# Layer 1 of a two-layer gated network: output stage ordered behind expert parts, per-query products in a narrower window, the last group's first expert products in five PSUM banks

## The chip, the cores and the metric

The kernel runs on one core of a Trainium2 chip. The metric is the device time of one execution in microseconds. A measured time is the median of the runs given; the profile is one further execution.

## The reference

64 sequences of 128 tokens by 128 features, with a context of 77 by 128 each, pass through two layers of gated cross attention and a mixture of eight experts. Cut to what matters here, the second layer is:

```python
x = x + tanh(g_xattn[1]) * L1_xattn(layernorm(x), ctx, ctx, ...)
x = x + tanh(g_ffn[1])   * L1_ffn(layernorm(x), Wg, W1, W2)

def L1_xattn(query, key, value, ...):        # 16 heads of 8
    scores = einsum('bhqd,bhkd->bhqk', q, k) + einsum('bhqd,qkd->bhqk', q, rel_k)
    attn = softmax(scores / sqrt(8))
    out = einsum('bhqk,bhkd->bhqd', attn, v) + einsum('bhqk,qkd->bhqd', attn, rel_v)
    return out @ Wo + bo

def L1_ffn(x, Wg, W1, W2):                   # 8 experts, hidden 256, top 2
    combine = ...                            # the two best probabilities, normalised
    h = square(relu(einsum('td,edh->teh', x, W1)))
    return einsum('te,ted->td', combine, einsum('teh,ehd->ted', h, W2))
```

Everything is float32 with tight accuracy, so matrix products with the experts' weights are made from a high and a low part.

## The kernel before, in words

The sequences go in 16 groups of four. In layer 1 each group passes through a pipeline whose stages lie in successive steps of one loop (`run`, L1120): step k runs the output stage (`l1_out`) and then the routing (`l1_route`) of group k-2, the attention proper (`l1_attend`) of group k-1, the projections (`l1_project`) and the per-query position products (`l1_relate`) of group k, and beside them the experts' parts (`l1_ffn`, through `tape`) of an earlier group.

The stages are Python generators. `weave` (L42) interleaves them: each stream has a row in `PLAN` with a window (start and end as shares of the step), a priority, and an entry "behind". Streams marked "experts" leave a mark after every part; a stream with a number n as its "behind" gets order edges, so that its TensorE instructions stand behind the experts' part n+1 marks back. An order edge is no semaphore wait; it only binds the order in which the scheduler may place instructions on TensorE. The program so traced goes through a scheduler that fixes the order of every engine's queue at build time with its own model of durations. On the chip each engine takes its queue in order, and so does SP, which issues most DMAs.

What the prediction touches, in the order in which the data of a group flows:

- `l1_rel` (L779): 32 queries by four, per-query products of q with the position table, in six chunks of two banks. ACT copies each bank to sg (L785) and stores it to DRAM (ra, L786).
- `l1_fetch` (L799): SP reads the products back, turned, as rq: four transfers per sequence, 16 per group.
- `l1_attend`: scores (L824) plus rq on DVE (L826), maximum (L827), subtraction on POOL (L828), transposes to the bank ST (L836), exp on ACT (L837), weighing by the values (L844). After all of them the relative-value products L884, in four chunks, each copied to rvs by DVE (L888). SP stores rvs to DRAM (rd, four transfers, L892) and reads it back as rp (L894).
- `l1_out`: the residual x is loaded (L903) and bo added on POOL (L904); rp is transposed on TensorE into po (L908), the rest of the attention is added (L910), divided (L912), transposed (L916) and projected (L922).
- `l1_project`: q, k and v products (L719) for the next group; `split3` makes three bfloat16 pieces; `stack_q` and `stack_k` store them (dq, L150; dk, L155) and SP reads them back as qst (L735) and kst (L747).
- `l1_ffn`: per expert two first products pz (L165 to L167 from L985, each product in three matmuls), squared relu (L988 to L992), high and low part (ACT L995, POOL L996), the expert's scores spread over the partitions (pb, L608) and copied to sb by ACT (L613), the second product py, and its sum (L622, L623). First products have two banks (tag "gu"); pb and py share one bank (tag "y"). The copy sb and the bank "misc" have one buffer each. At a group's end `flush` (L587 to L589) turns the sum and stores it.

Of the kernel before, what the change touches and what calls it, by code (L numbers as in the profile page):

```python
# [10 lines left out]
F32 = mybir.dt.float32  # L11
# [8 lines left out]
B, S, D = 64, 128, 128  # L20
# [21 lines left out]
def weave(tc, streams, marks=None):  # L42
# [31 lines left out]
    wei=(0, 0.7, 0, 6),  # L74
    max=(0.05, 0.8, 1000, None),
    fea=(0.2, 0.6, 500, None),
    out1=(0.25, 0.4, 600, None),
    att1=(0.1, 0.95, 0, None),
    rel1=(0.37, 0.93, 0, None),
    relT=(0.6, 0.9, 500, None),  # L80
    relL=(0.5, 0.8, 500, None),
    prj1=(0, 0.35, 0, None),
    t0=(0, 1.1, 0, "experts"),
    t1=(0, 1.15, 0, "experts"),
    attE=(0, 0.35, 500, None),
    tE=(0.1, 1.1, 0, "experts"),
    prjT=(0, 0.55, 1000, None),
# [7 lines left out]
class Spare:  # L95


    def __init__(self, pool, bufs):
        self.pool, self.bufs = pool, bufs

    def tile(self, shape, dt, tag, name):
        return self.pool.tile(shape, dt, tag="gu", bufs=self.bufs, name=name)


class Net:
# [496 lines left out]
        nc.scalar.copy(s3[:24], pp[:24, :GT])  # L602
        return s3

    def spread(self, w, s3):

        pb = self.pY.tile([128, 512], F32, tag="y", name="pb")
        self.nc.tensor.matmul(pb, lhsT=w, rhs=s3, start=True, stop=True)  # L608
        return pb

    def score_in(self, s3, e):
        sb = self.fp.tile([128, GT], F32, tag="sb", bufs=1, name="sb")
        self.nc.scalar.copy(sb, self.spread(self.sel[:, e : e + 1].to_broadcast([128, 128]), s3))  # L613
        return sb

    def add_expert(self, e, acc, py, sb):
# [314 lines left out]
    def l1_route(self, s):  # L931
# [32 lines left out]
        s["sd"] = self.scores_out(p)  # L964
        yield

    def l1_ffn(self, g, s):
        nc, a = self.nc, self.fp
        x3, xh, xl, sd = s["x"], s["xh"], s["xl"], s["sd"]
        acc = a.tile([128, GT], F32, tag="acc", bufs=2, name="acc")  # L970

        def down(e, hs):
            sb = self.score_in(sd, e)
            py = self.pY.tile([128, 512], F32, tag="y", name="py")
            for c, (m, hh, hl) in enumerate(hs):
                self.mm3(py, self.w2s[0][:, m], self.w2s[1][:, m], hh, hl, start=(c == 0), stop=(c == 1))
            self.add_expert(e, acc, py, sb)

        late = None
        for e in range(E):  # L980
            hs = []
            for c in range(2):
                m = slice((2 * e + c) * 128, (2 * e + c + 1) * 128)
                pz = self.pGU.tile([128, 512], F32, tag="gu", bufs=self.gub, name="pz1")
                self.mm3(pz, self.w1s[0][:, m], self.w1s[1][:, m], xh, xl)  # L985
                t = a.tile([128, GT], F32, tag="t", bufs=3, name="t")

                nc.scalar.activation(t, pz, AF.Relu)  # L988
                if c:
                    nc.vector.tensor_tensor(t, t, t, ALU.mult)  # L990
                else:
                    nc.scalar.activation(t, t, AF.Square)  # L992
                hh = a.tile([128, GT], F32R, tag="hh", bufs=3, name="hh")
                hl = a.tile([128, GT], F32R, tag="hl", bufs=3, name="hl")
                nc.scalar.copy(hh, t)  # L995
                nc.gpsimd.tensor_tensor(hl, t, hh.bitcast(F32), ALU.subtract)  # L996
                hs.append((m, hh, hl))
                yield
                if late:
                    down(*late)  # L1000
                    late = None
                    yield
                if e == 1 and c == 1:
                    self.flush()
            late = (e, hs)
        down(*late)
        self.pending = (acc, x3, self.out[4 * g : 4 * g + 4].rearrange("b p d -> p b d"))
        yield
# [147 lines left out]
    def next_layer(self):  # L1156

        tc = self.tc
        for cm in self.f0_open:
            cm.__exit__(None, None, None)  # L1160
        self.f0_open = None
        s2 = self.ctx1.enter_context(tc.tile_pool(name="psS2", bufs=1, space=PSUM))
        self.pGU = self.ctx1.enter_context(tc.tile_pool(name="psg1", bufs=1, space=PSUM))
        self.gub = 2
        self.banks = itertools.cycle(((self.pS, "S"), (s2, "S2"), (self.pST, "ST")))
        self.l1_ffn_setup(self.ctx1.enter_context(tc.tile_pool(name="f1", bufs=1)))
        self.ppcm, self.pp = self.pool("p1")
        self.l1_buffers(4)
# [87 lines left out]
```

## Time and profile before

| | |
|---|---|
| median of three runs | 2787.84 us (2786.68 to 2804.19) |
| profiled execution, its own time | 2781.41 us |
| its span, first to last instruction | 2779.7 us |
| mean granted TensorE clock | 0.934 |
| TensorE matmul, busy | 2403.1 us (86%) |
| VectorE (DVE), busy | 1949.9 us (70%) |
| ScalarE (ACT), busy | 1561.4 us (56%) |
| GpSimd (POOL), busy | 1545.5 us (56%) |
| chain that ended last, by engine | PE 49%, DMA 17%, DVE 15%, issue 6%, POOL 5%, SP queue 4%, ACT 3% |

The busy time of TensorE is modelled from pipelined matmuls, so a high share is no proof that TensorE is the bound. The chain that ended last is followed back from the last instruction, at each step to whatever released it; transfers have 17% of it. Layer 0 lasts to about 1340 us. Layer 1 follows, with steps of 76 to 84 us from about 1785 to 2575 us, and a tail in which the last groups have no other work beside them (from about 2690 us TensorE is busy 55 us of 80).

### The profile page before, as it was taken

The numbers are of one execution on the slowest core, as the hardware profiler recorded it, in microseconds if no ns is written. First come the engines' busy times: TensorE is split into PE (matmuls) and PEld (weight loads), VectorE is DVE, ScalarE is ACT, GpSimd is POOL, SyncE is SP. The second block draws the span as 40 slices with busy tenths as digits, with TensorE's granted clock in tenths as the row PEclk, the third lists the DMA queues.
The fourth block names the chain that finished last, engine by engine and source line by source line (L and its number), as shares of the span: only waits on it lengthen the run. The fifth ranks groups of instructions, "written<-read, shape, count | busy, mean of one in ns | idle before, by whom it ended". The sixth has DMA issues, their size and how long they took to land.

```text
span 2779.7 us, 61119 instructions
## 1 busy us (share of the span) xinstructions
PE 2403.1 (86%) x23638; PEld 1655.3 (60%) x23638; DVE 1949.9 (70%) x4054; ACT 1561.4 (56%) x3030; POOL 1545.5 (56%) x1508
## 2 busy tenths in 40 slices
PE   3788998898998998899886988889989888889876
PEld 2456666666666666666564555566666565656654
DVE  3378888888888888888764656656656666656566
ACT  2455655565655555565543545556656565656556
POOL 4455555555545565554645646655645665655556
PEclk9989999999999999999996899989999999999999
DMA  6744445534445534432434745565554566664510
GB/s 146 167 113 84 105 85 112 115 93 104 106 84 112 118 95 99 112 87 58 99 67 132 140 92 119 122 123 115 108 113 106 115 125 125 125 125 103 99 27 8
DMA packets 504414, 290.57 MB, mean 105 GB/s; under 512 B 264614, under 2 KB 480814, under 8 KB 504027
## 3 DMA queue, kind: packets, MB, share of 16 engines
q1 hardware_dynamic: 476475, 246.28, 43.8%
q10 hardware_dynamic: 27648, 40.38, 4.0%
q8 instruction: 186, 3.05, 0.5%
q14 instruction: 105, 0.86, 0.1%
HBM read 147.19 MB, written 138.60 MB: 103 GB/s over the span
## 4 chain that ended last, share of the span: by engine, by line
PE 49%; DMA 17%; DVE 15%; issue 6%; POOL 5%; SPq 4%; ACT 3%; DVEq 0%; POOLq 0%; ACTq 0%
PE py L165 4%; PE py L166 3%; DMA kst<-dk 3%; PE py L167 3%; PE ST L836 3%; DMA rp<-rd 3%; PE AV L385 2%; PE AV L844 2%; PE pg L165 2%; PE S L779 2%; DMA rq<-ra 2%; PE pu L165 2%; PE pg L166 2%; PE pg L167 2%; DVE sc L826 2%
## 5 line engine op out<-in xcount | busy, mean ns | idle before, releaser
L524 POOL TENSOR_TENSOR hl<-t,hh 128x512 fp32r<-128x512 f32 x336 | 442.8, 1321 | 362.5 <-ACT hh L523 348.9
L996 POOL TENSOR_TENSOR hl<-t,hh 128x512 fp32r<-128x512 f32 x256 | 347.1, 1368 | 219.9 <-ACT hh L995 216.6
L523 ACT CAST hh<-t 128x512 fp32r<-128x512 f32 x336 | 207.3, 617 | 175.4 <-PE py L167 74.2
L828 POOL TENSOR_TENSOR sc<-sc,mx 128x308 f32<-128x308 f32 x256 | 187.4, 737 | 189.6 <-DVE mx L827 145.0
L516 ACT ACTIVATE t<-pg 128x512 f32<-128x512 f32 x336 | 201.0, 598 | 151.0 <-PE pg L167 105.5
L517 DVE SCALAR_TENSOR_TENSOR t<-t,pg 128x512 f32<-128x512 f32 x336 | 227.9, 678 | 75.1 <-ACT t L516 74.5
L613 ACT COPY sb<-pb 128x512 f32<-128x512 f32 x256 | 150.0, 586 | 192.3 <-PE pb L608 191.5
L518 DVE TENSOR_TENSOR t<-t,pu 128x512 f32<-128x512 f32 x336 | 227.5, 677 | 14.9 <-PE pu L167 6.3
L837 ACT ACTIVATE rel<-ST 77x512 f32<-77x512 f32 x256 | 158.4, 619 | 123.6 <-PE ST L836 120.4
L826 DVE TENSOR_TENSOR sc<-S,rq 128x308 f32<-128x308 f32 x256 | 119.9, 473 | 153.3 <-PE ST L836 57.1
L622 DVE TENSOR_TENSOR ys<-sb,py 128x512 f32<-128x512 f32 x224 | 152.7, 682 | 86.3 <-PE py L167 80.9
L995 ACT CAST hh<-t 128x512 fp32r<-128x512 f32 x256 | 156.8, 625 | 58.9 <-PE py L167 48.4
L836 PE MATMUL ST<-ident,sc 128*128 128x128 f32 (+1 forms) x1024 | 171.5, 293 | 16.0 <-ACT rel L837 6.3
L399 ACT ACTIVATE P<-ST 77x512 f32<-77x512 f32 x256 | 151.0, 591 | 55.9 <-PE ST L396 53.4
L165 PE MATMUL pg<-xh,wg_h 128*128 128x512 f32 x336 | 160.4, 477 | 15.0 <-DVE t L518 13.9
L165 PE MATMUL py<-hh,wd_h 128*128 128x512 f32 x336 | 156.6, 466 | 18.9 <-ACT sb L613 12.5
L358 DVE TENSOR_REDUCE mx<-S 128x5 f32<-128x385 f32 (+1 forms) x192 | 110.3, 577 | 78.5 <-PE S L355 77.4
L165 PE MATMUL pu<-xh,wu_h 128*128 128x512 f32 x336 | 159.2, 474 | 5.8 <-DVE t L517 5.6
L988 ACT ACTIVATE t<-pz 128x512 f32<-128x512 f32 x256 | 151.4, 597 | 22.4 <-POOL hl L996 21.1
L836 PEld LDWEIGHTS ST<-ident,sc 128*128 128x128 f32 (+1 forms) x1024 | 123.4, 149 | 56.3 <-issue 13.4
L785 ACT COPY sg<-S 128x385 f32<-128x385 f32 (+1 forms) x192 | 91.6, 515 | 114.0 <-PE S L779 108.1
L166 PE MATMUL py<-hl,wd_h 128*128 128x512 f32 x336 | 147.8, 440 | 2.1 <-POOL hl L524 2.1
(248 smaller groups left out, 6582.8 us busy)
## 6 DMA issues: line engine op xcount, KB each, us to landing
rq<-ra SPq DMA_DIRECT2D x256, 154.0 KB
qst<-dq SPq DMA_DIRECT2D x96, 384.0 KB
ra<-sg ACTq DMA_DIRECT2D x128, 192.5 KB
kst<-dk SPq DMA_DIRECT2D x96, 231.0 KB
dq<-f SPq DMA_DIRECT2D x47, 384.0 KB
od<-av SPq DMA_DIRECT2D x32, 512.0 KB
ra<-sg ACTq DMA_DIRECT2D x64, 231.0 KB
dq<-f SPq DMA_DIRECT2D x47, 256.0 KB
```

The costliest lines, as they stand in the source:

```text
L165: nc.tensor.matmul(ps, lhsT=wh, rhs=xh, start=start, stop=False)
L166: nc.tensor.matmul(ps, lhsT=wh, rhs=xl, start=False, stop=False)
L516: nc.scalar.activation(t, pg, AF.Tanh, scale=0.5)
L517: nc.vector.scalar_tensor_tensor(t, t, 1.0, pg, ALU.add, ALU.mult)
L518: nc.vector.tensor_tensor(t, t, pu, ALU.mult)
L523: nc.scalar.copy(hh, t)
L524: nc.gpsimd.tensor_tensor(hl, t, hh.bitcast(F32), ALU.subtract)
L826: nc.vector.tensor_tensor(sc, sp[:, :, :KL], rqs[b][:, hg], ALU.add)
L828: nc.gpsimd.tensor_tensor(sc, sc, m.unsqueeze(2).to_broadcast([128, 4, KL]), ALU.subtract)
L836: nc.tensor.transpose(st[:r, j, :], sc.rearrange("q j k -> q (j k)")[:, j * KL : j * KL + r], self.ident)
L837: nc.scalar.activation(relg[:KL, hg, b], st[:KL].rearrange("k j (q e) -> k j q e", e=2), AF.Exp, scale=1.0 / math.sqrt(HD))
L996: nc.gpsimd.tensor_tensor(hl, t, hh.bitcast(F32), ALU.subtract)
```

## The change

Three rows of the plan are altered. The output stage (`out1`) gets order edges behind the experts' parts (its "behind" goes from none to 2). The window of the per-query products (`rel1`) ends at 0.78 of the step and not at 0.93. The window of the experts' parts (`t1`) ends at 1.25 and not at 1.15. For the last group alone, the first expert products rotate over the two "gu" banks and the three banks that the attention used (S, S2, ST), and the spread of the scores goes to the bank "misc" and not to the bank "y" that the second products use.

```diff
-    out1=(0.25, 0.4, 600, None),
+    out1=(0.25, 0.4, 600, 2),
-    rel1=(0.37, 0.93, 0, None),
+    rel1=(0.37, 0.78, 0, None),
-    t1=(0, 1.15, 0, "experts"),
+    t1=(0, 1.25, 0, "experts"),
...
-    def __init__(self, pool, bufs):
-        self.pool, self.bufs = pool, bufs
+    def __init__(self, pool, bufs, tag="gu"):
+        self.pool, self.bufs, self.tag = pool, bufs, tag
     def tile(self, shape, dt, tag, name):
-        return self.pool.tile(shape, dt, tag="gu", bufs=self.bufs, name=name)
+        return self.pool.tile(shape, dt, tag=self.tag, bufs=self.bufs, name=name)
...
-    def spread(self, w, s3):
-        pb = self.pY.tile([128, 512], F32, tag="y", name="pb")
+    def spread(self, w, s3, last=False):
+        pool, tag = (self.pmisc, "misc") if last else (self.pY, "y")
+        pb = pool.tile([128, 512], F32, tag=tag, name="pb")
...
+    def zbank(self, g):
+        return next(self.tailz) if g == self.ng - 1 else Spare(self.pGU, self.gub)
...
-            sb = self.score_in(sd, e)
+            sb = self.score_in(sd, e, g == self.ng - 1)
...
-                pz = self.pGU.tile([128, 512], F32, tag="gu", bufs=self.gub, name="pz1")
+                pz = self.zbank(g).tile([128, 512], F32, tag="gu", name="pz1")
...
+        gu = Spare(self.pGU, self.gub)
+        self.tailz = itertools.cycle((gu, Spare(self.pS, 1, "S"), gu, Spare(s2, 1, "S2"), gu, Spare(self.pST, 1, "ST")))
```

More of the change, by code (lines that the diff above doesn't have):

```diff
@@ L603, in scores_out, with score_in @@
         return s3
-    def spread(self, w, s3):
-        pb = self.pY.tile([128, 512], F32, tag="y", name="pb")
+    def spread(self, w, s3, last=False):
+        pool, tag = (self.pmisc, "misc") if last else (self.pY, "y")
+        pb = pool.tile([128, 512], F32, tag=tag, name="pb")
         self.nc.tensor.matmul(pb, lhsT=w, rhs=s3, start=True, stop=True)
         return pb
-    def score_in(self, s3, e):
+    def score_in(self, s3, e, last=False):
         sb = self.fp.tile([128, GT], F32, tag="sb", bufs=1, name="sb")
-        self.nc.scalar.copy(sb, self.spread(self.sel[:, e : e + 1].to_broadcast([128, 128]), s3))
+        self.nc.scalar.copy(sb, self.spread(self.sel[:, e : e + 1].to_broadcast([128, 128]), s3, last))
         return sb
```

## The prediction

> **What bounds the kernel now.** I read the page's shares first: TensorE is busy 86% of the span and the chain that ended last names several engines and DMA, so no single engine is the bound and the stage has to be asked. Only the second layer is touched (the first ends near 1340 us), so the next view is TensorE's waits in its steady part, eleven steps from 1770 to 2640 us. Columns: engine and line, what it waited for, total us, times, longest.
>
> ```profile
> PE po L908 <- DMA rp<-rd: 56.1, 11, 7.0
> PE S L824 <- DVE sc L826: 11.6, 13, 1.3
> PE pp L599 <- POOL p3b L138: 10.3, 11, 1.0
> PE S L824 <- DVE avt L855: 6.2, 11, 0.6
> ```
>
> One wait stands out: 56.1/11 = 5.1 us per step in which TensorE stands before the output stage's first transposes (L908), because the relative-value result rp is not back from DRAM. The timeline of TensorE shows it in one step:
>
> ```profile
> 2255.03 0.60 PE L836 MATMUL ST<-ident,sc 128*128 128x128 f32 x4
> 2261.19 1.11 PE L908 MATMUL po<-ident,rp 128*128 128x128 f32 x4 [5.56 <-DMA rp<-rd]
> ```
>
> Why rp is late is in SP's queue in that step (start, time taken, line, transfer, count):
>
> ```profile
> 2230.68 7.42 SPq L799 DMA_DIRECT2D rq<-ra  x10
> ...
> 2241.46 4.84 SPq L892 DMA_DIRECT2D rd<-rvs  x4
> ...
> 2254.03 0.79 SPq L894 DMA_DIRECT2D rp<-rd  x1
> 2254.86 1.63 SPq L735 DMA_DIRECT2D qst<-dq  x2
> 2258.88 2.38 SPq L747 DMA_DIRECT2D kst<-dk  x2
> ```
>
> SP takes one transfer after another. I measure from T0, the end of the step's last relative-value product (L884; 2235.0 here). The score fetches (rq) start at T0-4.3, the stores of the product (rd) go out at T0+6.5, rp is asked for at T0+19.1 and is there at T0+26.2. Over the eleven steps that end with the L908 at 1785.7 to 2575.5, rp is there 26.1 to 28.6 us after T0, mean 26.9, and a step is 78 us long.
>
> **The change, part by part.** The diff only shifts planner numbers; the built order of each engine's instructions tells what moves.
>
> *Output stage behind the experts.* In a steady step of before, 120 TensorE instructions lie between the last L884 and L908; in the changed order 87, in twelve steps alike. L908 moves forward, against what the words suggest. It loses 14 split products (0.235 us start to start in the timeline: 3.3), 2 projections (0.55 each for 308 columns: 1.1), 8 score transposes (0.13: 1.0), 4 weighing products (0.4), 4 score products (0.3), 1 score spread (0.3): 6.4 us of cover. Before, TensorE needs 20.7 us from T0 to L908, 1.0 of it waits; so it would arrive 13 to 14 us after T0. The 6.4 us of work are not gone, they follow L908. So a step changes by 6.4 us plus the shift of rp's landing against T0: break-even is a landing at T0+26.9-6.4 = T0+20.5.
>
> *Per-query products closer together.* They (L779) now end earlier against T0: the order puts 64 more L884 products (2 x 1.08 us), 6 split products of py (1.45), 3 of pz (0.75), a q projection (0.97) and smaller work between them and T0, 13.9 us by the rows' start-to-start times, against 5.5 before. The last two chunks' copies to sg (0.49 each) and the stores to ra (0.35; 3.3 from issue at 2227.36 to the first rq) follow, so the rq fetches start about 5 us after the last L779, at T0-8.9 instead of T0-4.1. That is the gain. On SP, however, the queue order changes too. From the first rq to rd: before 14 transfers, 10.8 us, 0.77 each; after 19 (12 rq, 3 dq, the output store, 3 dk), 14.6 us. Then rd and x (4.9 + 0.5), and now both qst and both kst go ahead of rp (1.6 + 2.4). rp is asked for at T0-8.9+24.0 = T0+15.1, four us earlier than before, but behind 1.2 MB of qst and kst. In the trace's DMA records of the step at 2254, the packets of qst (1,536 of 512 B) pass from 2257.9 to 2264 and those of kst (1,536 of 308 B) up to 2268, in queue order and with all engines full: 10 us, beginning 3 us after the issue. With qst asked for at T0+11.1, rp can pass at T0+24 and is there at about **T0+25**. From below: rp 5.0 us after its issue, as in the step at 2646.8 with nothing behind it: T0+20. From above: SP no faster per transfer than before (0.89 over 27) and 7.7 us to land plus the queue: T0+28. I take 25 because the packets' order is seen.
>
> TensorE's wait then grows from 5.1 to some 11 us, and a step gains 25 - 26.9 + 6.4 = **+4.5 us** (bounds -0.5 and +7.5). What hides behind that wait costs nothing: POOL's addition of bo (L904) is now ahead of seven other POOL operations and waits for x, asked for between the rd stores at T0+8 and there 4.75 us later (2252.49 to 2257.24 before); with L904's 1.26 and the four or five POOL operations that TensorE needs before L908 (0.7 to 1.3 each) it can't be at L908 before about T0+19; the DVE copies of L884's results now stand behind the k split (L135, L137), under half a us. The granted clock is 0.50 in 2258 to 2264 around the wait, and also around waits of only 3.3 us (1869 to 1875), so that loss stays in both kernels: 0.
>
> Twelve steps have this order; the step after it (no next projection; 17.4 us to L908, no wait before) loses the same 6.7 us of cover with 16 rq ahead of rd, so I count it as the thirteenth: 13 x 4.5 = +58 us.
>
> The Trainium skill ("DMA: Bandwidth & Descriptors", "Anatomy of one DMA") gives a transfer about 2 us plus its bytes over 436 GB/s, fitted on another issue path; for rp's 256 KB that would be an estimated 2.6 us, a landing at T0+17.7 and a change of some -40 us in all. The trace speaks against it for this place: rp takes 4.9 to 7.7 us from issue to use in the steps of full size.
>
> *Last group's products in five banks, its score spreads in another bank.* This touches only the last 40 us. There TensorE pays, per expert, a spread and the wait for its copy:
>
> ```profile
> 2767.13 0.38 PE L608 MATMUL pb<-s,sel 128*128 128x512 bf16 x1 [0.85 <-DVE ys L622]
> 2768.18 0.50 PE L165 MATMUL py<-hh,w2s_h 128*128 128x512 f32 x1 [0.68 <-ACT sb L613]
> ```
>
> From spread to spread 3.56 us (2767.13 to 2770.69). With the spread in its own bank 0.38 + 0.68 = 1.06 us can leave this chain, at most 8 x 1.06 = 8.5. But POOL has two subtractions (1.28 to 1.7) and half an addition per expert, some 3.5 us, which is late next while first products remain. The five banks end waits of 0.3 to 1.0 us on ACT (L988) that POOL would then hold. I take **-5 us** (-1 to -9).
>
> Sum: +58 - 5 = +53 us on the profiled execution's own 2781.41 us (span 2779.7 and 1.7 around it). The three timed runs' median, 2787.84, lies 6.4 above; the difference carries over: **2841 us**.
>
> **Rivals.**
> *The earlier fetches win (not slower).* The rq fetches begin 4.8 us earlier against T0 and four of them move behind rp. If DMA catches up while TensorE works, rp lands at or before T0+20.5, and from there on the step is not longer. For it: DMA share is only 0.45 to 0.8 at 2243 to 2255, so there is room; at 2646.8 rp lands at T0+17.3. Against it: that step has no qst and kst ahead. At T0+20 the steps give 13 x (-0.5) = -7, with the tail -12: 2776; with the other small waits (28 us in the view above) half gone, about 2765.
> *Partly so.* rp at T0+21 to 22: 13 x 0.5 to 1.5 less 5: +2 to +15, 2790 to 2803.
> *SP and DMA both slow.* With 12 rq, 3 dq and 3 dk in a row the queue is full when rd comes; rp at T0+28: 13 x 7.5 - 5 = +93, 2881.
> *The change does what it says.* L908 is covered and the 5.1 us go: 13 x -5.1 - 5 = -71, 2717. The built order speaks against it, since L908 has less work ahead of it, not more; only a landing at T0+15 would do it.
>
> **How the numbers follow.** Forecast (rp at T0+23 to 27, +26 to +80 us with the tail) 0.62; partly 0.12; earlier fetches win 0.12, half of it beyond 1%; slow queue 0.12; as said 0.02. About 1% (28 us) is what a measurement of this kernel can tell from no change. Slower by over 1%: forecast, nearly whole, and slow queue, 0.73. Faster by over 1%: 0.08. The rest, 0.19, within. The range, from the not-slower bound of the steps (2776) to the slow queue (2881) with the tail's 4 us on either side: 2772 to 2885.
>
> **What would show it.** TensorE's wait at the output stage's first transposes: 8 to 13 us per step instead of 5.1, arriving under 20 us after the last L884; SP with both qst and kst ahead of rp; a step of about 82 us; the last group's experts at about 3 us instead of 3.56. I am wrong if rp lands under 20 us after the last L884, or if a wait in the denser per-query products (on ACT's sg copies) is larger than the one at rp.

## The result, and the profile after

| | before | after |
|---|---|---|
| median of the timed runs | 2795.11 us (4 runs, 2786.68 to 2804.19) | 2831.03 us (4 runs, 2824.06 to 2834.84) |
| profiled execution, its own time | 2781.41 us | 2834.84 us |
| its span | 2779.7 us | 2833.1 us |
| mean granted TensorE clock | 0.934 | 0.929 |
| TensorE matmul, busy | 2403.1 us (86%) | 2417.5 us (85%) |
| DMA in the chain that ended last | 17% | 22% |
| SP's queue in that chain | 4% | 8% |

The ratio is 1.0125, with a 95% interval of 1.0079 to 1.0171: the changed kernel is slower by 22 to 48 us. The two profiled executions lie 53.4 us apart, more than the medians (35.9 us): the one before is 5 us under the lowest of its four timed runs, the one after is the highest of its four. Of the 53.4 us, 8.2 are there before the first L908 of layer 1 (1496.3 against 1504.5 us), in code that the change doesn't touch. That is scatter: the order of every engine up to that point is the same in both traces, and the profiled executions of six kernels below, which don't alter it either, reach it at 1494.0 to 1503.2 us. So 45 us belong to layer 1: 49.7 us more from the first use of rp to the last (1198.5 against 1248.2 us), and 4.5 us less from there to the end (84.9 against 80.4 us). Of the 49.7 us, 33.0 lie in the ten steady steps that follow here, 6.4 ahead of them and 10.3 behind them, where TensorE waits 9.0 us for rp at 2694.9 and before waited none.

The steady steps, from one first use of rp to the next, take 79.0 us before (ten steps, 1785.7 to 2575.5) and 82.3 us after (ten steps, 1800.3 to 2623.0). TensorE's waits in these steps of the changed kernel (columns as before: what waited, for what, total us, times, longest; lines from L780 on have moved by one):

```profile
PE po L909 <- DMA rp<-rd: 75.4, 11, 9.1
PE S L885 <- DVE avt L856: 21.3, 10, 2.6
PE S L825 <- DVE sc L827: 8.0, 20, 0.6
PE ST L837 <- POOL sc L829: 5.0, 3, 3.7
```

The wait for rp has grown from 5.1 to 6.9 us a step. Beside it stands a new one, 2.1 us a step at the relative-value products (L885). The wait at pp (L599, 10.3 us before) is gone from this list.

One step on TensorE and on SP, by their timelines (start, time taken, line, operation, in brackets the idle time and what ended it). T0, the end of the last relative-value product, is 2191.7 here:

```profile
2184.50 2.15 PE L885 MATMUL S<-rel,rv 128*32 128x64 f32 x66 [2.62 <-DVE avt L856]
...
2205.21 0.48 PE L845 MATMUL AV<-rel,vb 128*32 128x128 f32 x8
2212.17 1.12 PE L909 MATMUL po<-ident,rp 128*128 128x128 f32 x4 [6.48 <-DMA rp<-rd]
```

```profile
2176.52 4.54 SPq L800 DMA_DIRECT2D rq<-ra  x8
...
2192.61 1.50 SPq L893 DMA_DIRECT2D rd<-rvs  x2
...
2195.51 1.97 SPq L893 DMA_DIRECT2D rd<-rvs  x2
2197.51 3.20 SPq L736 DMA_DIRECT2D qst<-dq  x2
2200.76 1.79 SPq L748 DMA_DIRECT2D kst<-dk  x2
2202.66 2.47 SPq L895 DMA_DIRECT2D rp<-rd  x1
```

The score fetches start 15 us ahead of T0 instead of 4, rd goes out at T0+1, rp is asked for at T0+11.0 and used at T0+20.5. But it is asked for behind qst and kst, and the time from its request to its use is 9.5 us, where before it was 6.1 to 7.7 us.

The windows of the same step (stretch, its length, busy time of TensorE, weight load, DVE, ACT, POOL with counts, then the granted clock, the DMA share and GB/s) show what surrounds the two waits:

```profile
2183.00:2186.00 3.00, 1.50 (x56) 1.50 (x60) 2.17 (x7) 0.52 (x1) 1.09 (x2) 0.64 1.23 217
2186.00:2189.00 3.00, 3.00 (x25) 2.25 (x16) 1.61 (x3) 0.52 (x1) 0.83 (x2) 0.50 1.26 221
...
2207.00:2210.00 3.00, 0.00 (x0) 0.00 (x0) 0.00 (x0) 0.00 (x0) 1.09 (x2) 0.62 1.20 142
2210.00:2213.00 3.00, 0.83 (x5) 0.83 (x5) 0.00 (x0) 0.00 (x0) 0.00 (x0) 0.50 1.29 174
2213.00:2216.00 3.00, 3.00 (x16) 1.68 (x14) 2.26 (x3) 0.62 (x1) 1.90 (x2) 0.50 0.42 57
```

Between 2207 and 2212 all four compute engines are nearly idle while the DMA share is 1.20 and more (a packet counts with all its time in the stretch where it starts, so the share can pass 1): the step waits for data. The clock falls to 0.50 around each of the two waits.

### The profile page after: what moved, and what is told of

Read it like the earlier page. It is cut to its first block, busy times and chain, and to the rows that moved or that the text cites. A ratio compares the mean times of both kernels' runs of the same rounds, so it can differ in the third digit from the quotient of the medians.

```text
span 2833.1 us, 61114 instructions
## 1 busy us (share of the span) xinstructions
PE 2417.5 (85%) x23638; PEld 1666.5 (59%) x23638; DVE 1955.8 (69%) x4054; ACT 1562.3 (55%) x3030; POOL 1555.7 (55%) x1508
## 4 chain that ended last, share of the span: by engine, by line
PE 43%; DMA 22%; DVE 13%; SPq 8%; POOL 6%; issue 6%; ACT 2%; ACTq 0%; DVEq 0%; POOLq 0%
DMA kst<-dk 4%; DMA rp<-rd 4%; PE py L165 3%; PE py L166 3%; PE py L167 3%; PE ST L837 3%; PE S L780 3%; DMA dk<-f 2%; PE AV L385 2%; PE AV L845 2%; PE pg L165 2%; PE pu L165 2%; POOL f L138 2%; DVE ln_xn L128 2%; PE pg L166 1%
## 5 line engine op out<-in xcount | busy, mean ns | idle before, releaser
L167 PE MATMUL py<-hh,wd_l 128*128 128x512 f32 x336 | 143.0, 425 | 0.0
```

What stands on the lines that cost most here:

```text
L167: nc.tensor.matmul(ps, lhsT=wl, rhs=xh, start=False, stop=stop)
```

## The experiments

All ratios are to the kernel before, with 95% intervals. "Step" is the mean from one first use of rp to the next in the profiled execution, "landing" the first use of rp after T0 where TensorE waits for it.

The order edge of the output stage has no run of its own. With that edge alone the built order of all five engines is that of the kernel before, so there is nothing to time. The other two plan edits each change the order.

### One plan edit at a time

The window of the per-query products alone:

```diff
-    rel1=(0.37, 0.93, 0, None),
+    rel1=(0.37, 0.78, 0, None),
```

> The kernel before with one number altered, the end of the per-query products' window (0.93 to 0.78). Its built order has the changed kernel's steady step. Theory (the narrower window carries the whole loss): rp 20 to 24 us after the last relative-value product, TensorE's wait at its first use 6 to 8 us a step, a second wait of about 2 us a step at the relative-value products, steps of 82 to 82.5 us against 79.0; and no gain at the end, so 35 to 45 us above before, ratio 1.013 to 1.016. Rival (the order edge or the experts' longer window matter on the chip): steps of 79 to 80 us, ratio under 1.005.

Measured: 2835.09 us, ratio 1.0143 (1.0109 to 1.0177); step 82.2 us; from the last use of rp to the end 85.0 us. TensorE's waits in it, same columns:

```profile
PE po L908 <- DMA rp<-rd: 75.5, 11, 8.5
PE S L884 <- DVE avt L855: 21.2, 10, 2.6
```

Both waits of the changed kernel are there, at the same size. This one number carries the whole loss.

The experts' window alone:

```diff
-    t1=(0, 1.15, 0, "experts"),
+    t1=(0, 1.25, 0, "experts"),
```

> The kernel before with the experts' window alone ending at 1.25. Its built order differs from both kernels': 119 TensorE instructions (about 18 us of work) between the last relative-value product and the first use of rp, as before, but on SP twelve score fetches and three stores of q ahead of the stores of rd, and qst ahead of rp. Theory (the wait goes by what SP has ahead of rp): rp at 26 to 28 us after the last relative-value product, wait of 5 to 8 us, steps 79 to 82 us, ratio 1.000 to 1.015. Rival (the wait goes by the cover on TensorE alone): rp and wait as before, steps 79 us, ratio 1.000.

Measured: 2831.04 us, ratio 1.0133 (1.0100 to 1.0165); step 81.9 us, landing 27.5 to 30.6 us, wait 82.1/11 = 7.5 us:

```profile
PE po L908 <- DMA rp<-rd: 82.1, 11, 8.8
```

TensorE reaches the first use of rp 20.5 us or more after T0, so it has as much cover as before, and still waits 2.4 us longer. rp is asked for at T0+20 to 24 here (mean 21.8, before 20.0), behind fifteen score fetches and the loads qst, which before stand behind it, and is used at T0+28.8 on average instead of 26.9. So the cover alone doesn't decide; what is new ahead of rp is qst. Together the two windows cost no more than either: with both, the order is the one that the narrower per-query window gives.

The last group's banks alone, with all three plan rows as before:

> The changed kernel with the plan of before, so that only the last group's five banks and the moved score spreads are new. Theory: steps of 79.0 us as before, and 80.4 us from the last product of the output stage to the end against 84.9: -4 to -5 us, ratio 0.998. Rival (the shorter end in the changed kernel comes from its other order, not from the banks): 84 to 85 us there, ratio 1.000.

Measured: 2791.85 us, ratio 0.9989 (0.9966 to 1.0013), which can't be told from no change; step 79.2 us, and 82.9 us from the last use of rp to the end, between the two expectations. The place of the gain is clearer: from the transposes of the last group's routing weights (L599) to the end it is 44.1 us before, 43.7 us with the narrower window alone, 40.3 us in the changed kernel and 39.7 us here. From L599 to the first of the last eight spreads of the scores it is 5.2 and 5.4 us without the banks, 1.3 and 2.0 us with them. So the banks give about 4 us, and how early the weights are there (40 to 43 us after the last use of rp) moves the rest.

### The queue ahead of rp

The loads of qst and kst ordered behind rp, in the changed kernel:

```diff
+            with self.behind_rp():
-            nc.sync.dma_start(out=qst[64 * r : 64 * r + 48],
+                nc.sync.dma_start(out=qst[64 * r : 64 * r + 48],
...
+            with self.behind_rp():
-            nc.sync.dma_start(out=kst[64 * r : 64 * r + 48],
+                nc.sync.dma_start(out=kst[64 * r : 64 * r + 48],
...
+    def behind_rp(self):
+        return self.tc.issue_after(self.last_rp.ins) if self.last_rp else nullcontext()
```

> The changed kernel with the loads qst and kst ordered behind rp on SP. The planner then also moves the first use of rp forward, to some 7 to 9 us of TensorE work after the last relative-value product (12.5 in the changed kernel). Theory (qst and kst ahead of rp cost about 4 us on SP and the rest in transfer time): rp there 15 to 18 us after the last relative-value product, wait 6 to 9 us, and the step no longer than the changed kernel's; with 4 us less cover and 5 us earlier rp about 81 to 82 us, total -5 to -15 us against the changed kernel, ratio to before 1.005 to 1.012. Rival (the transfer takes its time wherever it stands, score fetches included): rp at 20 to 22, wait 11 to 13, step 85 us or more, ratio over 1.02.

Measured: 2794.14 us, ratio 0.9996 (0.9973 to 1.0019), 37 us less than the changed kernel; step 79.7 us (by turns 75 to 77 and 80 to 84); landing 12.5 to 15.5 us, wait 46.1/11 = 4.2 us. This is better than the theory had it, which gave a landing at T0+15 to 18 and 5 to 15 us less: rp is used 2.8 to 3.3 us after its request. TensorE still waits, since the new order brings it to rp 8.7 to 10.5 us after T0.

So in the next run the first use of rp was held back to where the changed kernel has it:

```diff
-    out1=(0.25, 0.4, 600, 2),
+    out1=(0.27, 0.4, 600, 2),
...
+            if 2 < self.step_no < self.ng:
+                self.tc.add_manual_dep(t.ins, self.last_av.ins.name, mybir.DependencyInfo(
+                    mybir.DependencyClass.NoSync, mybir.DependencyReason.DATA), reason="order")
```

Here t is the transpose of rp and last_av the last weighing product traced so far; an edge of this kind is an order, not a wait.

> The changed kernel with qst and kst ordered behind rp, and the first use of rp held back (an order edge to a weighing product, and the output stage's window from 0.27), so that it has about 12 to 14 us of TensorE work ahead of it again, as in the changed kernel. Against the changed kernel only the queue ahead of rp is new. Theory (the wait is qst and kst on the queue, no more): rp asked for at 10 to 11 us and there at 13.5 to 14.5 us after the last relative-value product, TensorE there at 14 to 15 us, wait under 1 us; with the 6.9 us and part of the clock's fall gone steps of 74.5 to 76.5 us and 75 to 100 us less than the changed kernel, ratio to before 0.977 to 0.987. Rival (what TensorE doesn't wait for here it waits for elsewhere: qst and kst late at the next scores, POOL or DVE behind): steps of 79 us or more, ratio 0.998 or more.

Measured: **2751.76 us, ratio 0.9869 (0.9817 to 0.9921)**, 79 us less than the changed kernel and faster than both kernels. In the eight steps from 2022.7 to 2603.8 us, the step is 72.6 us, and TensorE arrives 12.3 to 15.2 us after T0. Its waits from 2022.7 to 2530.4 us:

```profile
PE S L893 <- DVE avt L864: 8.9, 6, 2.0
PE S L832 <- DVE sc L834: 7.8, 14, 1.0
...
PE po L917 <- DMA rp<-rd: 1.4, 2, 1.1
```

SP's queue in one of these steps (T0 = 2298.4):

```profile
2303.24 2.52 SPq L901 DMA_DIRECT2D rd<-rvs  x2
2310.26 0.33 SPq L903 DMA_DIRECT2D rp<-rd  x1
2310.64 1.28 SPq L742 DMA_DIRECT2D qst<-dq  x2
2311.96 2.32 SPq L755 DMA_DIRECT2D kst<-dk  x2
```

The last rd store is issued by 2305.8, and rp is asked for only at 2310.3, when rd has reached DRAM. In the changed kernel SP issues qst and kst in just that gap. They cost the request for rp about one us; what they cost is the data queue behind which rp then stands.

The dose between the two: only kst behind rp, qst ahead again, the rest as in the run before. In the steady steps the orders on TensorE and on DVE are the same in both traces, and SP's queue differs only in the place of rp against qst.

```diff
-            with self.behind_rp():
-                nc.sync.dma_start(out=qst[64 * r : 64 * r + 48],
+            nc.sync.dma_start(out=qst[64 * r : 64 * r + 48],
```

> As the run with the window from 0.27, but only kst stands behind rp; qst goes ahead of it again. The order on TensorE is the same, so this is the dose between the changed kernel (both ahead: rp there 21.5 us after the last relative-value product, 8.6 us after its issue) and that run (none ahead: 14 us, 2.9 us after its issue). Theory (rp waits for the data queued ahead of it; qst has 0.79 MB of the 1.25): rp there at 17 to 19 us, wait 3 to 5 us, steps of 76 to 79 us, ratio to before 0.99 to 1.003. Rival (the place on SP alone counts, some 1.5 us for qst): rp at 15 to 16 us, wait 0 to 1, steps under 75.5 us, ratio under 0.99.

Measured: 2797.62 us, ratio 0.9989 (0.9966 to 1.0011). Its waits from 2022 to 2500 us, and SP's queue in one step (T0 = 2321.2):

```profile
PE po L916 <- DMA rp<-rd: 23.3, 7, 4.2
```

```profile
2325.51 1.95 SPq L900 DMA_DIRECT2D rd<-rvs  x2
2327.50 3.59 SPq L741 DMA_DIRECT2D qst<-dq  x2
2332.07 0.33 SPq L902 DMA_DIRECT2D rp<-rd  x1
```

The three kernels beside each other, in like steps (after 2046.6 to 2539.1 us, kst alone behind rp 2027.6 to 2497.0, both behind rp 2022.7 to 2530.4), in us; TensorE arrives at T0+14 to 15 in all three:

| ahead of rp on SP | rp asked for | rp's request to use | landing or use | wait | clock time lost per step | step |
|---|---|---|---|---|---|---|
| qst and kst (changed kernel) | T0+12.4 | 8.9 | T0+21.3 | 7.0 | 5.2 | 82.1 |
| qst | T0+10.9 | 7.0 | T0+17.9 | 3.3 | 4.9 | 78.2 |
| neither | T0+11.6 | 3.2 | T0+14.7 | 0.2 | 1.2 | 72.5 |

The clock time lost is one less the granted clock, times the length, over the same stretch. Over the ten steady steps it is 5.2 us a step in the kernel before and 5.1 in the changed kernel; single steps scatter from 2.4 to 9.4 us. With qst ahead, rp is asked for as early as with neither and is still there 3.8 us later in its transfer: so the theory of the data queue holds and that of the place on SP falls. From the first row to the second the step loses 3.9 us and the wait 3.7, but the order on TensorE is another one there, so this is no clean dose of kst. From the second to the third, where rp's place on SP alone is new, the step loses 5.7 us, of which the wait is 3.1 and the clock up to 3.7.

Two more runs put the same question to the plan of before, and to a longer cover with rp first. The plan of before with the new banks, qst and kst behind rp, has the wide per-query window, so all sixteen score fetches still stand ahead of rp. But in the steady steps of the kernel before qst and kst stand behind rp as it is:

> The plan of before and the last group's five banks, with qst and kst ordered behind rp; the window of the per-query products is the old, wide one. All sixteen score fetches now stand ahead of rp, four of them behind the stores of rd, and 18.6 us of TensorE work lie between the last relative-value product and rp's first use. Theory (score fetches ahead of rp cost as qst and kst do, so that the wide window is what keeps before from 73 us): rp at 21 to 24 us, wait 2 to 4 us, steps of 76.5 to 79 us, ratio 0.985 to 1.000. Rival (qst and kst are the whole matter, the window none): rp under 19 us, wait under 0.5, steps of 73 to 75 us, ratio under 0.984.

Measured: 2784.01 us, ratio 0.9940 (0.9905 to 0.9976); step 78.9 us. SP's queue in one step (T0 = 2243.8):

```profile
2250.81 4.82 SPq L900 DMA_DIRECT2D rd<-rvs  x4
...
2260.66 1.53 SPq L807 DMA_DIRECT2D rq<-ra  x3
...
2263.78 1.18 SPq L902 DMA_DIRECT2D rp<-rd  x1
```

rp lands at T0+25 to 29, later than the 21 to 24 expected, and the wait is 55.6/10 = 5.6 us. In these steps SP's queue and the orders of the other engines are those of the kernel before (and of the run with the banks alone, 0.9989), so the run repeats it and tests nothing there. What it shows is that qst and kst don't hold rp up in the kernel before. That the score fetches do is likely, since all sixteen of them stand ahead of rp, but not shown. The changed plan, with rp first and its first use held back, has 72.6 us a step against 78.9; how much of that is the narrow window's wasn't tried apart.

The run that reached 2751.76 us, with the output stage's window from 0.33 to 0.42, which gives the first use of rp about 19 us of TensorE work:

> The same with the window from 0.33: some 19 to 20 us of TensorE work ahead of the first use of rp. Theory: no wait there, and nothing more to be had than with 13 us: steps of 74.5 to 76.5 us, ratio 0.977 to 0.987. Rival (later output stage makes the experts of the group late): 77 us or more, ratio over 0.99.

Measured: 2792.98 us, ratio 1.0006 (0.9983 to 1.0029); step 79.1 us, with no wait for rp in any of these steps. The rival's numbers hold; whether late experts are the cause, as it says, wasn't followed. TensorE comes to rp 21 to 34 us after T0 where the work ahead of it was counted at 19, so other waits have taken its place; their single causes were not followed.

### More cover instead of another queue

```diff
-    out1=(0.25, 0.4, 600, 2),
+    out1=(0.45, 0.55, 600, 2),
...
-    rt1=(0.45, 0.7, 1000, None),
+    rt1=(0.6, 0.85, 1000, None),
```

and the edge of the transposes behind the last weighing product, in the changed kernel:

> The changed kernel with the first use of rp held back to 28 to 30 us of TensorE work after the last relative-value product (window of the output stage 0.45 to 0.55, of the routing 0.6 to 0.85); on SP the planner then has rp directly behind rd. Cover instead of order of the queue. Theory: no wait, clock as in the undisturbed parts, steps of 74.5 to 76.5 us, ratio 0.977 to 0.987. Rival (the later output stage holds the residual, the routing and the experts back): 78 us or more, ratio over 0.995.

Measured: 2814.87 us, ratio 1.0076 (1.0044 to 1.0108); step 81.1 us, no wait for rp in these steps. The same on the plan of before (with no entry "behind" for the output stage) and with the new banks:

> The plan of before with the last group's five banks, and the first use of rp held back to about 30 us of TensorE work as in the run before this. Theory (the 5.1 us that before waits, and the clock's fall behind that wait, are to be had by cover alone): wait 0, steps of 73 to 75.5 us, with the banks' gain ratio 0.975 to 0.985. Rival: a wait for the next thing (POOL's additions, the stores to ra) takes its place, steps of 78 us or more, ratio over 0.99.

Measured: 2789.80 us, ratio 0.9989 (0.9965 to 1.0014); step 80.1 us. My theory fell in both. TensorE reaches rp 34 to 46 us after T0, where the work in between was counted at 28 to 30, and other waits have come in. In the second, from 1770 to 2560 us:

```profile
PE S L825 <- DVE sc L827: 23.6, 19, 2.6
PE po L587 <- DVE acc L620: 10.0, 10, 1.1
PE S L780 <- DMA qst<-dq: 7.3, 9, 1.8
```

Its TensorE is idle 7.9 us a step, against 8.7 in the kernel before and 5.1 in the kernel of 2751.76 us; its granted clock in these steps is 0.94 (0.93 before, 0.97 there). Why the later output stage spreads the wait rather than ends it was not followed further, and stays open.

### The second wait of the changed kernel

L885 waits for the copy avt (L856), since DVE does the next group's layer norm first:

```profile
2182.29 1.94 DVE L128 TENSOR_SCALAR xg<-xg,ln_mv,ln_rs 128x128 f32<-128x128 f32 x4 [0.59 <-POOL ln_rs L123]
2184.15 0.29 DVE L856 COPY avt<-S 128x144 f32<-128x144 f32 x1
```

An order edge on DVE puts L128 behind that copy:

```diff
+            if w == "a" and self.step_k - 2 in self.avts:
+                self.tc.add_manual_dep(t.ins, self.avts[self.step_k - 2], mybir.DependencyInfo(
+                    mybir.DependencyClass.NoSync, mybir.DependencyReason.DATA), reason="order")
```

> The changed kernel with one order edge on DVE: the next group's normalised input (L128) stands behind the last avt copy that TensorE waits for, instead of ahead of it. The orders of TensorE and SP stay those of the changed kernel. Theory (the chain runs from the last per-query product over SP's fetches to rp; what ends earlier before the last relative-value product is waited for at rp): the wait at the relative-value products falls from 2.1 to under 0.7 us, the one at rp grows by as much, to 8 or 9 us, steps of 81.5 to 82.5 us, within 8 us of the changed kernel, ratio to before 1.010 to 1.016. Rival (a cost of its own, with a fall of the clock behind it): steps of 79 to 80.5 us, ratio 1.000 to 1.006.

Measured: 2827.64 us, ratio 1.0092 (1.0068 to 1.0116), an interval that overlaps the changed kernel's; step 82.5 us. Its waits from 1770 to 2640 us:

```profile
PE po L915 <- DMA rp<-rd: 88.4, 11, 9.7
PE ST L842 <- POOL sc L834: 13.1, 10, 3.3
```

The wait at the relative-value products is no longer among them, and the one at rp is 8.0 us instead of 6.9, rp's landing T0+22.5 to 24.8 instead of T0+19.7 to 24.6. What ends earlier is waited for at rp, as the theory said.

The same edge in the kernel of 2751.76 us, where nothing waits for rp:

> The run with the window from 0.27 and rp ahead of qst and kst, with the DVE order edge of the run before this. Theory (without the wait at rp the step is set by TensorE and what feeds it, so the wait of 1.5 us at the relative-value products now counts): steps 0.5 to 2 us shorter than 73.3, 5 to 20 us less in all, ratio 0.980 to 0.986. Rival (the copy isn't what that step waits for): the same, 0.987, or slower by the new order.

Measured: 2769.13 us, ratio 0.9885 (0.9857 to 0.9913). In the last seven full steps it has 72.7 us a step against 72.6 without the edge; the four steps ahead of them, where its order differs, take 335.8 us against 318.6. The rival holds: that copy isn't what this step waits for in the end.

## Why the prediction was right, and where not

2841 us was forecast and 2831.03 us measured, inside the range of 2772 to 2885, on the side of slower that had the 0.73. The forecast's sum was +53 us on the profiled execution: +58 in the steps, -5 at the end. The two traces show +45 in layer 1: +49.7 and -4.5. The timed medians lie 35.9 us apart (22 to 48), so a rise of 53 was too much. That the totals differ by only 10 us is in part luck: the forecast started from 2787.84 us, the median of three runs, and with a fourth run the median before is 2795.11.

**Which window does it, and the order on TensorE.** The built order was the right thing to read. TensorE arrives at rp T0+14.0 to 14.8 (13 to 14 predicted) and the output stage moves forward rather than behind the experts. The narrower window alone gives the loss.

**SP's queue.** 19 transfers lie between the first score fetch and rd, and qst and kst go ahead of rp, as predicted. rp is asked for at T0+12.4 instead of T0+15.1. From the last per-query product to rp's landing the prediction has 13.9 + 25 = 38.9 us; measured over the ten steps from 1800.3 to 2539.1 us it is 38.2 us, 16.8 of them ahead of T0. The chain that sets the step was sized right to 0.7 us.

**The landing against T0, and the wait.** Measured from T0 the same landing is T0+21.5, not T0+25, and the wait 6.9 us, not 11. That lies outside the band that the forecast gave (T0+23 to 27) and beside the rival "partly so", by whose sum the whole would have been some +8 us. The step that failed is the break-even at T0+20.5, with its condition that nothing but the 6.4 us of moved work changes between a landing and the next T0. By that sum a landing at T0+21.5 makes the step 21.5 - 26.9 + 6.4 = 1.0 us longer; measured it is 3.3. From a use of rp to the next T0 it is 52.0 us before and 60.8 after, 8.7 more instead of 6.4. TensorE's waits in this stretch are 3.6 us a step instead of 2.1, most of them for the copy avt (2.1 us each at L885, where before it held the scores, L824, for 0.6).

The run with DVE's edge shows that the two errors are one. It has the orders of the changed kernel on TensorE and SP, and without the wait for avt the stretch is 58.6 us, 6.6 more than before, which is the moved work. The landing is T0+23.9 (mean of the nine steps from 1867.1 to 2528.4), inside the band, and the sum then gives 23.9 - 26.9 + 6.4 = 3.4 us, where 3.5 are measured. So the copy held T0 back by about two us, which made the landing look that much earlier and the wait at rp smaller, and left the step as it was. A step was forecast 4.5 us longer and is 3.3, since even without that wait rp lands 1.1 us ahead of T0+25. That the step itself came out at the forecast's "about 82 us" is luck in part: it was added to 78 us, where the ten steps before mean 79.0. The clock's loss, put at "0", holds over ten steps: 5.2 us a step before, 5.1 after.

**The size for qst and kst.** From qst's request to rp's landing the prediction has 25 - 11.1 = 13.9 us; it is 14.4 us in the seven steps of the table. The dose runs show what of it rp would be spared: 3.8 us in its transfer for qst, and 1.9 for kst, where the order on TensorE differs too. The lower bound for rp, 5.0 us after its issue "with nothing behind it", was no bound. TensorE doesn't wait at that use of rp (2646.8), so 5.0 us is when TensorE came, not when rp landed; with neither qst nor kst ahead rp takes 2.8 to 3.7 us.

**The Trainium skill's price.** The formula of "DMA: Bandwidth & Descriptors", "Anatomy of one DMA", which is fitted on another issue path, gives an estimate of 2.6 us for rp's 256 KB. In the two kernels with qst and kst behind rp and the narrow window it takes 3.2 and 3.0 us from request to use, so the page is near the chip here. The 8.9 us of the changed kernel are mostly queue.

**POOL's addition of bo.** I had POOL unable to reach the output stage before T0+19. Wrong: in the kernel of 2751.76 us, with rp used at T0+14.7, TensorE doesn't wait there for POOL. In the changed kernel x was asked for at T0+2.5 in the step shown, not at T0+8.

**The end.** -5 predicted, -4.5 measured, but not by experts 3 us apart: the last eight spreads of the scores take 29.6 us from the first to the last, and 29.9 before. The whole series starts 4.5 us earlier, 41.5 against 46.0 us after the last use of rp. Whether its own bank or the five banks of the first products bring it forward wasn't tried apart.

**The rivals.** That the earlier fetches win was nearer than its 0.12: rp did land 5.4 us earlier against T0, one us short of the break-even. What kept it from winning is shown by the dose, with the first use of rp held at T0+14 to 15: with kst moved away the kernel equals before, with both moved away it is 1.3% faster.

## What to carry to other kernels

Ask of a transfer on the path not only when its request is issued, but how many bytes stand ahead of it on its queue; a load that goes out in a gap of the issuing engine looks free there and is paid for by the next one. A wait is best measured as one chain, from the last product that starts the transfers to the product that uses them: a point on another engine between the two (T0 here) moves with the order. A wait that is covered by other work isn't gone with certainty: three kernels that come to rp only 21 to 46 us after T0, and don't wait for it in their steady steps, were no faster than before. The two that were faster have rp early, ahead of qst and kst, and come to it 12 to 16 us after T0 in most of their last seven full steps.

## What the runs showed of the hardware

Ending the last 3 us of wait gave 5.7 us a step, with the same orders on TensorE and DVE. The windows of one step of the kernel of 2751.76 us, around its use of rp, against those of the changed kernel above (columns as there):

```profile
2236.00:2239.00 3.00, 3.00 (x27) 1.98 (x26) 2.83 (x5) 2.38 (x4) 3.00 (x3) 1.00 0.15 17
2239.00:2242.00 3.00, 3.00 (x26) 1.87 (x25) 1.89 (x4) 2.59 (x5) 3.00 (x4) 1.00 0.74 189
```

The granted clock stays at 1.00, where the changed kernel has 0.50 to 0.62 for 9 us. With kst alone behind rp the three waits shown by like steps differ: behind 4.2 us (2184.1) and 3.3 us (2339.0) the clock falls to 0.50 and 0.52, behind 3.1 us (2262.7) it stays at 1.00:

```profile
2184.00:2187.00 3.00, 2.93 (x10) 2.12 (x11) 1.29 (x2) 0.05 (x1) 1.01 (x1) 0.50 1.09 154
...
2262.00:2265.00 3.00, 2.27 (x14) 1.83 (x15) 1.42 (x3) 0.64 (x2) 1.93 (x2) 1.00 1.32 165
...
2340.00:2343.00 3.00, 3.00 (x11) 2.12 (x10) 1.60 (x4) 1.26 (x3) 2.49 (x2) 0.52 1.31 171
```

In both steps between them it also falls to 0.50 around the relative-value products. The kernel with neither ahead pauses there too, up to 2.0 us, and keeps 1.00 in the step shown; in three of its seven like steps it loses 1.7 to 3.4 us. Why it falls in some steps and not in others was not tried.

The Trainium skill ("TensorE: Matmul & The Clock Gate", "HAM oscillation — how this bites in real kernels") tells of a kernel whose array goes back to half rate at each wait for a transfer. The changed kernel's windows agree, with 0.50 around the wait for rp in the step shown.
